# Two states of 64 channels per scan tile, with the scan results kept in PSUM

## The chip, the cores and the metric

The kernel runs on one core of one Trainium2 chip. A core has five engines, each with its own queue of instructions: TensorE (PE, matrix products), VectorE (DVE), ScalarE (ACT), GpSimd (POOL) and SyncE (SP, which here issues all DMAs). An engine executes its queue in order and waits at an instruction until the semaphores named in it have reached their values. Data live in SBUF and, for results of matrix products and some intermediates, in PSUM[...]. The metric is device time in microseconds.

## The reference, cut to what matters

Two layers are computed on four images of 384 channels and 32x32 positions. The first half of each layer is a state-space scan. For every channel d, with 16 states n:

```
dA = exp(dt[d, t] * A[d, n])
h[d, n] = h[d, n] * dA + dt[d, t] * u[d, t] * B[n, t]
y[d, t] = sum over n of h[d, n] * C[n, t]
```

Layer 0 does this in four directions over the image (rows, columns, and both reversed) on 384 channels; layer 1 does it once on 768 channels between an input projection with a short convolution and an output projection. Both have layer norms around them. The second half of layer 0 is a small feed-forward net; that of layer 1 is a mixture of four experts, computed densely.

## The kernel before, in words

Positions are the columns of a tile, channels its partitions. A *pass* is one direction (or one half of layer 1's channels) of one image on 512 positions: 384 channels as three chunks of 128 partitions. There are 48 passes. Half of them start a sequence ("first"), the other half continue from kept states. A pass has 16 *steps*, one for each state n, so there are 768 steps. A step consists of

- `times_b` on POOL (L834): s = dtu * bt for all three chunks, where dtu is dt*u and bt is row n of B, spread over the partitions by a DMA;
- three times `decay` on ACT (L839): da = exp(dt * A[:, n]) into one of two separate PSUM tiles `das`, used in turn;
- three times `scan` on DVE (L848), in place in s, with da as the factor;
- in first passes `keep_state` on DVE (L860), which copies the last column of the three chunks;
- `times_c`: the product with row n of C. DVE does the first `share` chunks (L883), reading C from the PSUM tile pc, which PE fills by a small product (`spread_c`, L864); POOL does the others (L894), reading C from the SBUF tile ct, filled by a DMA;
- three times `add` on PE (L874): acc[:, c] += identity * s[:, c], so that the sum over n builds up in PSUM.

There are five s tiles, three bt and three ct tiles. After 16 steps `gather` (DVE) takes acc out. `prep_pass` makes dt and dtu of a pass ahead of time, `project` makes the rows of B and C, and jobs called `prep0`, `post0`, `prep1`, `post1` do the layer norms, projections and the feed-forward net of each image beside the scans ("side work").

The order of all this on each engine is written out by a planner (`Plan.run`): it keeps a clock per engine, gives every operation a cost (for instance 0.63 for a decay, 1.18 for a scan) and dependences, and emits at each turn the operation that starts first. `choose` lets side work in where it is not expected to delay a scan. `split` chooses `share` from how far POOL is ahead. The order is fixed when the program is built. Semaphore waits are then put in by the tile framework, from which instruction writes and reads which tile; the planner's own dependences do not become waits.

After the last scan and `post1` of the last image comes `moe_layer`, the four experts, in plain program order; it isn't touched.

Of the kernel before, what the change touches and what calls it, by code (L numbers as in the profile page):

```python
# [11 lines left out]
BF16 = mybir.dt.bfloat16  # L12
# [6 lines left out]
P = 128  # L19
NB = 4  # L20
D = 384
NC = D // P
# [13 lines left out]
CROWS = (64, 96)  # L36
NQ = 112
# [183 lines left out]
def conv_layers(ctx, tc, ins, x2, const):  # L221
# [24 lines left out]
    wx1 = wp.tile([P, NI, NQ], F32, name="wx1")  # L246
# [7 lines left out]
    dts = tiles(2, [P, NC, T], "dt")  # L254
    dtus = tiles(2, [P, NC, T], "dtu")
    xds = tiles(2, [64, L], "xd")
    c3s = tiles(2, [NQ, L], "c3", BF16)
    dtws = tiles(2, [64, D], "dtw")
    wxs = tiles(2, [P, NC, NQ], "wx")
# [9 lines left out]
    das = tiles(2, [P, T], "da", pool=ps_1)  # L269
    pc = ps_1.tile([P, T], F32, name="pc")  # L270
# [14 lines left out]
    pick = wp.tile([NQ, NS], BF16, name="pick")  # L285
    nc.vector.tensor_copy(pick, ident[:NQ, :NS])
    for at in CROWS:
        nc.vector.tensor_tensor(pick, pick, ident[:NQ, at : at + NS], ALU.add)

    a0 = wp.tile([P, 4 * NC, NS], F32, name="a0")  # L290
    a1 = wp.tile([P, NI, NS], F32, name="a1")
# [19 lines left out]
    def part(dram_ap, c, h):  # L311
        return dram_ap[c * P : (c + 1) * P, cols(h)]
# [45 lines left out]
    def project(q, h, px):  # L358


        xd, c3 = q["xd"], q["c3"]
        lo, hi = CROWS
        yield ACT, 0.6
        nc.scalar.copy(c3[:, cols(h)], px[:NQ])
        yield ACT, 0.6
        nc.scalar.copy(xd[:, cols(h)], px[:64])
        yield DVE, 0.65
        nc.vector.tensor_tensor(px[lo:NQ], px[lo:NQ], c3[lo:NQ, cols(h)], ALU.subtract)
        yield ACT, 0.6
        nc.scalar.copy(c3[lo:NQ, cols(h)], px[lo:NQ])  # L370
        yield DVE, 0.65
        nc.vector.tensor_tensor(c3[hi:NQ, cols(h)], px[hi:NQ], c3[hi:NQ, cols(h)], ALU.subtract)  # L372
        ps.give(px)
# [7 lines left out]
    def prep_pass(q, h, slot, u, u_view):  # L381

        dt, dtu = dts[slot], dtus[slot]
# [18 lines left out]
        for c in range(NC):  # L402
            yield POOL, 1.35
            nc.gpsimd.tensor_tensor(u_view(dtu[:, c, :]), u_view(dt[:, c, :]), u[:, c], ALU.mult)  # L404

# [21 lines left out]
    def prep_quad0(q, b, k):  # L427
        def gen():
# [4 lines left out]
            for h in range(NT):  # L433
                px = yield from ps.take(True)
                yield PE, 2.75
                at = u[:, :, cols(h)] if k % 2 == 0 else turned(u, h)
                for c in range(NC):
                    nc.tensor.matmul(px[:NQ], lhsT=q["wx"][:, c, :], rhs=at[:, c], start=c == 0, stop=c == NC - 1)  # L438
                yield from project(q, h, px)
# [5 lines left out]
    def prep_pass0(q, b, k, h, slot):  # L445
        def gen():
            u = st[("u0", b)]
            if k % 2 == 0:
                yield from prep_pass(q, h, slot, u[:, :, cols(h)], lambda t: t)
            else:  # L450
                yield from prep_pass(q, h, slot, turned(u, h), lambda t: t.rearrange("p (w h) -> p w h", h=HW))

        return gen
# [17 lines left out]
    def post0(b):  # L471
# [15 lines left out]
        def add_x(h):  # L487
            def gen():
                for c in range(NC):
                    xh = yield from t1.take()  # L490
                    yield SP, LOAD
                    nc.sync.dma_start(out=xh, in_=part(x_in[b], c, h))
# [141 lines left out]
    def prep_quad1(q, b, g):  # L634
        def gen():
# [6 lines left out]
            for h in range(NT):  # L642
                px = yield from ps.take(True)
                yield PE, 5.5
                for c in range(NI):
                    nc.tensor.matmul(
                        px[:NQ], lhsT=wx1[:, c, :], rhs=xc[c // NC][:, c % NC, cols(h)], start=c == 0, stop=c == NI - 1
# [7 lines left out]
    def prep_pass1(q, b, g, h, slot):  # L655
        def gen():
            xc = st[("xc", b)][g]
            yield from prep_pass(q, h, slot, xc[:, :, cols(h)], lambda t: t)
# [10 lines left out]
    def post1(b):  # L669
# [28 lines left out]
        def out(h):  # L698
            def gen():
# [21 lines left out]
                for m in range(NC):  # L721
                    xh = yield from t1.take()
                    yield SP, LOAD
                    nc.sync.dma_start(out=xh, in_=part(x1[b], m, h))
# [19 lines left out]
    for m, (layer, b) in enumerate(order):  # L744
# [4 lines left out]
        for k, h, first, rev in of:  # L749
            if first:  # L750
                shared = st.get((1, b, 0)) if layer == 1 else None
                if not shared:
# [7 lines left out]
                    "c3": shared["c3"] if shared else c3s[n_quads % 2],  # L760
# [31 lines left out]
    for p, (m, layer, b, k, h, first, rev) in enumerate(passes):  # L792
# [6 lines left out]
        deps = [("quad", p if first else p - 1)] + ([("gather", p - 2)] if p > 1 else [])  # L799
        jobs.append((("pass", p), deps, p, [of_pass(q, b, k, h, p % 2)]))  # L800
# [24 lines left out]

    def load(i, of, ring):
        p, n = steps[i]
        nc.sync.dma_start(
            out=ring[i % len(ring)], in_=quad(p)["rows"][of + n : of + n + 1, cols(passes[p][4])].partition_broadcast(P)
        )  # L830

    def times_b(i):
        p, n = steps[i]
        nc.gpsimd.tensor_tensor(ss[i % NSR], dtus[p % 2], rep(bts[i % NBR]), ALU.mult)  # L834

    def decay(i, c):
        p, n = steps[i]
        q = quad(p)
        nc.scalar.activation(  # L839
            das[(NC * i + c) % 2], dts[p % 2][:, c, :], AF.Exp, scale=q["a"][:, q["c0"] + c, n : n + 1]  # L840
        )

    def scan(i, c):
        p, n = steps[i]
        _, _, _, _, _, first, rev = passes[p]
        way = slice(None, None, -1) if rev else slice(None)
        s = ss[i % NSR]
        nc.vector.tensor_tensor_scan(  # L848
            s[:, c, way],
            das[(NC * i + c) % 2][:, way],  # L850
            s[:, c, way],
            0.0 if first else state[:, n, c : c + 1],
            ALU.mult,
            ALU.add,
        )

    def keep_state(i):
        p, n = steps[i]
        last = 0 if passes[p][6] else T - 1
        nc.vector.tensor_reduce(state[:, n, :], ss[i % NSR][:, :, last : last + 1], AX.X, ALU.max)  # L860

    def spread_c(i):
        p, n = steps[i]
        nc.tensor.matmul(  # L864
            pc,
            lhsT=pick[:, n : n + 1].to_broadcast([NQ, P]),
            rhs=quad(p)["c3"][:, cols(passes[p][4])],
            start=True,
            stop=True,
        )  # L870

    def add(i, c):
        n = steps[i][1]
        nc.tensor.matmul(acc[:, c, :], lhsT=ident, rhs=ss[i % NSR][:, c, :], start=n == 0, stop=n == NS - 1)  # L874
# [5 lines left out]
    def times_c(i):  # L880
        m = share[i]
        s = ss[i % NSR]
        nc.vector.tensor_tensor(s[:, :m, :], s[:, :m, :], rep(pc, m), ALU.mult)  # L883
        plan.end["split", i] = 0.0
        for c in range(m):
            plan.end["part", i, c] = plan.end["mult", i]
        if m == NC:
            plan.skip.add(("c", i))
            plan.end["c", i] = plan.end["mult", i]

    def times_c_pool(i):
# [3 lines left out]
        for c in range(m, NC):  # L895
            plan.end["part", i, c] = plan.end["c", i]

    main, gathers, decays, bs, cs, pcs, bl, cl = ([] for _ in range(8))
    adds = [[] for _ in range(NC)]
    where = {}  # L900
    for i in range(N):
        p, n = steps[i]
        first = passes[p][5]
        after = ("state", i) if first else ("scan", i, 2)
        ring = [("add", i - NSR, c) for c in range(NC)] if i >= NSR else []
        bl.append(Op(("bt", i), LOAD, [("quad", p if first else p - 1)] + ([("b", i - NBR)] if i >= NBR else []), lambda i=i: load(i, NS, bts)))
        cl.append(Op(("ct", i), LOAD, [("quad", p if first else p - 1)] + ([("c", i - NCR)] if i >= NCR else []), lambda i=i: load(i, 0, cts)))
        bs.append(Op(("b", i), 3.42, [("pass", p), ("bt", i), *ring], lambda i=i: times_b(i)))
        for c in range(NC):
            x = NC * i + c - 2  # L910
            decays.append(
                Op(("da", i, c), 0.63, [("pass", p)] + ([("scan", x // NC, x % NC)] if x >= 0 else []), lambda i=i, c=c: decay(i, c))
# [389 lines left out]
```

## Time and profile before

| | |
|---|---|
| median of 3 runs | 6793.34 us (6784.1 to 6800.1) |
| profiled execution | 6791.07 us, span 6789.3 us |
| first scan starts, last scan starts | 79.7 us, 4503.0 us |
| DVE busy | 4097.3 us, 60% of the span |
| POOL busy | 4095.7 us, 60% |
| PE busy | 5920.9 us, 87% |
| ACT busy | 2838.5 us, 42% |
| DMA | 494.99 MB, 24.3% of 16 engines' span |

The span has two parts. To about 4.5 ms the scans run; then, up to 6.79 ms, the experts keep PE busy without a break while DVE and POOL stand nearly still. Shares of the whole span are therefore means over two stages. In a row of a group the first number after the bar is busy time in us, the second the mean length of one instruction in ns, and after the second bar stands the idle time of the engine just before these instructions, with what ended it.

### The profile page before, as it was taken

Reading aid. Unit: us, or ns where it says so; the run is one execution under the profiler, and the core shown is the slowest. Engines: PE = TensorE matmul, PEld = TensorE weight load, DVE = VectorE, ACT = ScalarE, POOL = GpSimd, SP = SyncE. Lnnn points to the kernel's source line nnn. Section 1 sums busy time; section 2 is a strip of 40 time slices with the busy share of each in tenths; the row PEclk is TensorE's granted clock in tenths of the full one; section 3 lists DMA queues with packets and bytes.
Section 4 is the critical chain, followed back from the end, with each engine's and each line's share of the span. In section 5 each row is a group of like instructions: output and inputs, shape, how many; then the busy total and the mean of one; then the engine's idle time right before and its main releaser. Section 6 shows DMA issues by size and latency. Waiting matters only on the chain. (4 is left out here: it accounts for less than half of the span.)

```text
span 6789.3 us, 43235 instructions
## 1 busy us (share of the span) xinstructions
PE 5920.9 (87%) x13120; PEld 2424.6 (36%) x13120; DVE 4097.3 (60%) x4047; ACT 2838.5 (42%) x3991; POOL 4095.7 (60%) x1760
## 2 busy tenths in 40 slices
PE   6777798978888987888897898877899999999999
PEld 2222233323333332333333233333444444444444
DVE  6999888898999889899988884951100000000000
ACT  4445565656555555655555555542211111111111
POOL 5999988998989788999988884960000000000000
PEclk8999999999999999999999899998899999999999
DMA  3333323333334333333433332423000000000000
GB/s 91 104 103 104 100 88 100 97 108 98 107 102 122 101 93 106 99 109 109 120 99 94 98 92 62 123 76 114 0 0 0 28 0 0 28 0 0 10 14 14
DMA packets 302859, 494.99 MB, mean 73 GB/s; under 512 B 38240, under 2 KB 82336, under 8 KB 302624
## 3 DMA queue, kind: packets, MB, share of 16 engines
q1 hardware_dynamic: 302624, 492.22, 24.3%
q8 instruction: 103, 1.69, 0.1%
q14 instruction: 132, 1.08, 0.1%
HBM read 470.61 MB, written 21.50 MB: 72 GB/s over the span
## 5 line engine op out<-in xcount | busy, mean ns | idle before, releaser
L834 POOL TENSOR_TENSOR s<-dtu,bt 128x1536 f32<-128x1536 f32 x768 | 2638.5, 3444 | 169.5 <-PE acc L874 95.7
L874 PE MATMUL acc<-s,ident 128*128 128x512 f32 x4608 | 2296.1, 630 | 122.7 <-POOL s L894 110.6
L839 ACT ACTIVATE da<-dt,a 128x512 f32<-128x512 f32 x2304 | 1580.3, 690 | 1608.1 <-DVE s L848 1605.2
L874 PEld LDWEIGHTS acc<-s,ident 128*128 128x128 f32 x4608 | 895.5, 199 | 1870.3 <-issue 1525.3
L848 DVE TENSOR_TENSOR_SCAN s<-da,state,s 128x512 f32<-128x512 f32 x1152 | 1401.6, 1266 | 119.4 <-ACT da L839 104.0
L848 DVE TENSOR_TENSOR_SCAN s<-da,s 128x512 f32<-128x512 f32 x1152 | 1336.5, 1206 | 168.1 <-ACT da L839 115.3
L1201 POOL TENSOR_TENSOR xb<-xb,yg 128x1536 f32<-128x1536 f32 x32 | 119.1, 3723 | 1835.5 <-DVE yg L1198 1776.6
L894 POOL TENSOR_TENSOR s<-s,ct 128x512 f32<-128x512 f32 (+1 forms) x698 | 1058.9, 1518 | 218.2 <-issue 110.3
L1198 DVE SCALAR_TENSOR_TENSOR yg<-py,pvt,gate 128x512 f32<-128x512 f32 x96 | 66.2, 745 | 1850.4 <-PE py L1175 1848.2
L1175 PE MATMUL py<-hid,w 128*128 128x512 f32 x2304 | 1048.1, 593 | 1.1 <-DVE yg L1198 1.1
L1187 PE MATMUL ph<-tb,w 128*128 128x512 f32 x2304 | 1046.6, 592 | 0.0
L883 DVE TENSOR_TENSOR s<-s,pc 128x1024 f32<-128x1024 f32 (+2 forms) x768 | 882.2, 1149 | 61.9 <-PE pc L864 20.5
L1191 ACT ACTIVATE hid<-ph,pvt 128x512 f32<-128x512 f32 x384 | 263.8, 687 | 1521.5 <-PE ph L1187 1514.0
L864 PE MATMUL pc<-c,pick 112*128 112x512 bf16 x768 | 303.6, 395 | 537.1 <-DVE s L883 534.6
L1175 PEld LDWEIGHTS py<-hid,w 128*128 128x128 f32 x2304 | 438.5, 190 | 555.2 <-issue 551.5
L1187 PEld LDWEIGHTS ph<-tb,w 128*128 128x128 f32 x2304 | 438.1, 190 | 552.2 <-issue 552.0
L580 PE MATMUL ps<-u,w 128*128 128x512 f32 x576 | 274.7, 622 | 12.6 <-DMA w<-in_w_in_dram 5.6
L388 PE MATMUL ps<-xd,dtw 12*128 12x512 f32 (+1 forms) x288 | 184.1, 734 | 29.4 <-ACT dt L397 14.3
L404 POOL TENSOR_TENSOR dtu<-dt,u 128x512 f32<-128x512 f32 x96 | 132.4, 1400 | 76.5 <-ACT dt L400 76.5
L580 PEld LDWEIGHTS ps<-u,w 128*128 128x128 f32 x576 | 114.0, 200 | 167.2 <-issue 137.7
L864 PEld LDWEIGHTS <-pick 112*128 112x128 bf16 x768 | 77.2, 100 | 236.7 <-issue 236.7
L438 PE MATMUL ps<-u,wx 128*112 128x512 f32 x192 | 140.8, 881 | 14.1 <-DVE c L372 7.8
(138 smaller groups left out, 3222.1 us busy)
## 6 DMA issues: line engine op xcount, KB each, us to landing
bt<-rows SPq DMA_DIRECT2D x768, 256.0 KB, 3.2
ct<-rows SPq DMA_DIRECT2D x768, 256.0 KB, 3.3
w<-in_w_dram SPq DMA_DIRECT2D x8, 2304.0 KB, 22.5
w<-in_w_in_dram SPq DMA_DIRECT2D x48, 192.0 KB, 3.7
w<-in_w_out_dram SPq DMA_DIRECT2D x48, 192.0 KB, 3.6
u<-in_x_dram SPq DMA_DIRECT2D x8, 768.0 KB, 8.5
t<-in_x_dram SPq DMA_DIRECT2D x24, 256.0 KB, 3.8
x<-yx SPq DMA_DIRECT2D x8, 768.0 KB
```

The costliest lines, as they stand in the source:

```text
L388: nc.tensor.matmul(pd, lhsT=q["dtw"][QROW : QROW + nr, c * P : (c + 1) * P], rhs=q["xd"][QROW : QROW + nr, cols(h)], start=True, stop=True,)
L580: nc.tensor.matmul(pi, lhsT=w[:, c, :], rhs=u[:, c, cols(h)], start=c == 0, stop=c == NC - 1)
L834: nc.gpsimd.tensor_tensor(ss[i % NSR], dtus[p % 2], rep(bts[i % NBR]), ALU.mult)
L839: nc.scalar.activation(das[(NC * i + c) % 2], dts[p % 2][:, c, :], AF.Exp, scale=q["a"][:, q["c0"] + c, n : n + 1])
L848: nc.vector.tensor_tensor_scan(s[:, c, way], das[(NC * i + c) % 2][:, way], s[:, c, way], 0.0 if first else state[:, n, c : c + 1], ALU.mu ...
L864: nc.tensor.matmul(pc, lhsT=pick[:, n : n + 1].to_broadcast([NQ, P]), rhs=quad(p)["c3"][:, cols(passes[p][4])], start=True, stop=True,)
L874: nc.tensor.matmul(acc[:, c, :], lhsT=ident, rhs=ss[i % NSR][:, c, :], start=n == 0, stop=n == NS - 1)
L883: nc.vector.tensor_tensor(s[:, :m, :], s[:, :m, :], rep(pc, m), ALU.mult)
L894: nc.gpsimd.tensor_tensor(s[:, m:, :], s[:, m:, :], rep(cts[i % NCR], NC - m), ALU.mult)
L1175: nc.tensor.matmul(py[:, m, :], lhsT=w2[:, f, m * P : (m + 1) * P], rhs=hid, start=f == 0, stop=f == NF - 1,)
L1187: nc.tensor.matmul(ph, lhsT=w1[:, c, f * P : (f + 1) * P], rhs=ts[i][:, c, :], start=c == 0, stop=c == NC - 1)
L1191: nc.scalar.activation(hid, ph, AF.Gelu, bias=pv("b1", e * NF + f))
```

## The change

A scan tile of 128 partitions now holds two states of 64 channels instead of one state of 128 channels: partitions 0 to 63 have state 2m, partitions 64 to 127 state 2m+1. A pass has six groups of 64 channels; its 16 steps are two *parts* of eight: part 0 does groups 0 to 2 and part 1 groups 3 to 5, each for the eight pairs of states m. So a step still has three chunks x of 512 columns, and there are still 768 steps.

- `prep_pass` makes dt and dtu in the old layout (one tile each, shared by all passes) and copies them by DMA, SBUF to SBUF, into tiles dts and dtus with each group of 64 channels written twice: eight DMAs for each part, 16 for a pass.
- `load` takes two DMAs of 64 partitions for a bt or ct tile, one for each state.
- The three decays of a step go to the three parts of one PSUM tile `da`, which has three banks and exists once. The scan writes its result over da in PSUM (`in_psum`), and DVE multiplies it with ct from SBUF into s (`times_c`). Chunks that POOL multiplies are scanned into s as before[...].
- A step on DVE is now scan 0, scan 1, (state), product of the first chunks, scan 2, (state), and, where `share` is 3, a second product. `keep_state` is called twice a step in first passes.
- `add` uses `both`, a 128x64 matrix that sums the two halves, and writes 64 partitions of acc.
- `pc`, `spread_c` and the bfloat16 rows c3 that it needed are gone; `project` is one copy on ACT instead of three on ACT and two on DVE.

```diff
-    das = tiles(2, [P, T], "da", pool=ps_1)
-    pc = ps_1.tile([P, T], F32, name="pc")
+    da = ps_1.tile([P, NC, T], F32, name="da")
...
+    both = wp.tile([P, HP], F32, name="both")
+    nc.vector.tensor_tensor(both, ident[:, :HP], ident[:, HP:], ALU.add)
...
     def project(q, h, px):
+        nr = QROW + q["rank"]
         yield ACT, 0.6
-        nc.scalar.copy(c3[:, cols(h)], px[:NQ])
-        yield ACT, 0.6
-        nc.scalar.copy(xd[:, cols(h)], px[:64])
-        yield DVE, 0.65
-        nc.vector.tensor_tensor(px[lo:NQ], px[lo:NQ], c3[lo:NQ, cols(h)], ALU.subtract)
-        yield ACT, 0.6
-        nc.scalar.copy(c3[lo:NQ, cols(h)], px[lo:NQ])
-        yield DVE, 0.65
-        nc.vector.tensor_tensor(c3[hi:NQ, cols(h)], px[hi:NQ], c3[hi:NQ, cols(h)], ALU.subtract)
+        nc.scalar.copy(q["xd"][:nr, cols(h)], px[:nr])
         ps.give(px)
...
+    def until(*keys):
+        while not all(k in plan.end for k in keys):
+            yield None
+        return max(plan.end[k] for k in keys)
...
+        for part in range(2):
+            before = 0.0
+            if p:
+                before = yield from until(("scan", NS * (p - 1) + 8 * part + 7, 2))
+            for to, of in ((dts[part], dt), (dtus[part], dtu)):
+                yield SP, LOAD, before
+                for side in range(2):
+                    mine = [x for x in range(NC) if (3 * part + x) % 2 == side]
+                    chunks = [(3 * part + x) // 2 for x in mine]
+                    for k in range(2):
+                        nc.sync.dma_start(
+                            out=to[k * HP : (k + 1) * HP, mine[0] : mine[-1] + 1 : 2, :],
+                            in_=of[side * HP : (side + 1) * HP, chunks[0] : chunks[-1] + 1, :],
+                        )
+            plan.end["pass", p, part] = plan.now + LOAD + 2.0
...
     def load(i, of, ring):
-        p, n = steps[i]
-        nc.sync.dma_start(
-            out=ring[i % len(ring)], in_=quad(p)["rows"][of + n : of + n + 1, cols(passes[p][4])].partition_broadcast(P)
-        )
+        p, part, m = place(i)
+        for k in range(2):
+            row = of + 2 * m + k
+            nc.sync.dma_start(
+                out=ring[i % len(ring)][k * HP : (k + 1) * HP, :],
+                in_=quad(p)["rows"][row : row + 1, cols(passes[p][4])].partition_broadcast(HP),
+            )
...
-    def decay(i, c):
+    def decay(i, x):
...
-        nc.scalar.activation(
-            das[(NC * i + c) % 2], dts[p % 2][:, c, :], AF.Exp, scale=q["a"][:, q["c0"] + c, n : n + 1]
-        )
+        g = 2 * q["c0"] + 3 * part + x
+        nc.scalar.activation(da[:, x, :], dts[part][:, x, :], AF.Exp, scale=q["a"][:, g, m : m + 1])
...
-        s = ss[i % NSR]
+        s = ss[i % NSR][:, x, way]
+        d = da[:, x, way]
+        in_psum = x < share[i] if x else True
         nc.vector.tensor_tensor_scan(
-            s[:, c, way],
-            das[(NC * i + c) % 2][:, way],
-            s[:, c, way],
-            0.0 if first else state[:, n, c : c + 1],
-            ALU.mult,
-            ALU.add,
+            d if in_psum else s, d, s, 0.0 if first else state[:, j, x : x + 1], ALU.mult, ALU.add
         )
...
-        nc.tensor.matmul(acc[:, c, :], lhsT=ident, rhs=ss[i % NSR][:, c, :], start=n == 0, stop=n == NS - 1)
+        nc.tensor.matmul(
+            acc[side * HP : (side + 1) * HP, c, :],
+            lhsT=both,
+            rhs=ss[i % NSR][:, x, :],
+            start=m == 0,
+            stop=m == NS // 2 - 1,
+        )
...
-        nc.vector.tensor_tensor(s[:, :m, :], s[:, :m, :], rep(pc, m), ALU.mult)
+        nc.vector.tensor_tensor(ss[i % NSR][:, lo:hi, :], da[:, lo:hi, :], rep(cts[i % NCR], hi - lo), ALU.mult)
...
         for x in range(NC):
+            free = [("da free", i - 1) if x == 2 else ("mult", i - 1, 0)] if i else []
+            decays.append(Op(("da", i, x), 0.63, [("pass", p, part), *free], lambda i=i, x=x: decay(i, x)))
+            main.append(
+                Op(("scan", i, x), 1.12 if first else 1.18, [("da", i, x), ("b", i)], lambda i=i, x=x: scan(i, x))
+            )
+            if x == 0:
+                continue
+            if first:
+                main.append(Op(("state", i, x - 1), 0.12, [], lambda i=i, x=x: keep_state(i, x - 1)))
+            main.append(Op(("mult", i, x - 1), 1.11 if x == 1 else 0.62, [("ct", i)], lambda i=i, x=x: times_c(i, x - 1)))
```

## The prediction

> **What bounds the kernel now.** I read the page's slices first: DVE and POOL are at 8 to 9 tenths up to slice 27 and then nearly still, PE is at 9 to the end. So there is a scan stage and an expert stage, and only the scan stage is touched. The groups and the waits come next, then the timeline of a few steps. First the groups (the page's part 5) of a step's instructions:
>
> ```profile
> L834 POOL TENSOR_TENSOR s<-dtu,bt 128x1536 f32<-128x1536 f32 x768 | 2638.5, 3444 | 169.5 <-PE acc L874 95.7
> L839 ACT ACTIVATE da<-dt,a 128x512 f32<-128x512 f32 x2304 | 1580.3, 690 | 1608.1 <-DVE s L848 1605.2
> L848 DVE TENSOR_TENSOR_SCAN s<-da,state,s 128x512 f32<-128x512 f32 x1152 | 1401.6, 1266 | 119.4 <-ACT da L839 104.0
> L848 DVE TENSOR_TENSOR_SCAN s<-da,s 128x512 f32<-128x512 f32 x1152 | 1336.5, 1206 | 168.1 <-ACT da L839 115.3
> L864 PE MATMUL pc<-c,pick 112*128 112x512 bf16 x768 | 303.6, 395 | 537.1 <-DVE s L883 534.6
> ```
>
> ACT sits idle 1605 us for scans, DVE only 219 us for decays: the decays run ahead of DVE. The chain of waits says the same pair by pair:
>
> ```profile
> ACT da L839 <- DVE s L848: 1605.2, 1731, 7.7
> DVE s L848 <- ACT da L839: 219.3, 111, 6.4
> DVE s L848 <- POOL s L834: 66.5, 18, 22.3
> ```
>
> Lines of the timeline, DVE and then ACT:
>
> ```profile
> 1822.95 1.20 DVE L883 TENSOR_TENSOR s<-s,pc 128x1024 f32<-128x1024 f32 x1
> 1824.06 3.63 DVE L848 TENSOR_TENSOR_SCAN s<-da,state,s 128x512 f32<-128x512 f32 x3
> 1827.61 1.19 DVE L883 TENSOR_TENSOR s<-s,pc 128x1024 f32<-128x1024 f32 x1
> ```
>
> ```profile
> 1825.38 0.69 ACT L839 ACTIVATE da<-dt,a 128x512 f32<-128x512 f32 x1 [1.61 <-DVE s L848]
> 1826.55 0.69 ACT L839 ACTIVATE da<-dt,a 128x512 f32<-128x512 f32 x1 [0.48 <-DVE s L848]
> 1827.72 0.69 ACT L839 ACTIVATE da<-dt,a 128x512 f32<-128x512 f32 x1 [0.48 <-DVE s L848]
> ```
>
> The reader is to see that DVE has no hole: the product starts 0.08 us before the record of the scan ahead of it ends, and each decay is made while DVE scans the other da tile. A step takes 4.66 us here. DVE is the bound, POOL close behind it. Over the scan stage (79.7 to 4504 us, 4424 us) there are about 100 us in which all wait for the side work of the last image, and some 330 us of other waits on DVE.
>
> [...] The three parts of the new da are three banks, so the chip would let ACT fill one while DVE scans another, as the trace shows with the two old da tiles; any wait between parts comes from the program. [...] The trace prices it: an independent operation starts 0.083 us before the end of the one ahead, one that waits for it 0.034 us after (state behind scan: 2614.08 to 2614.11), or 0.11 where the wait stands in an instruction of its own.
>
> **The change part by part.** The deciding view is not in the trace of before. It is the list of waits in the program built from the changed kernel, beside that of the old one. In the old program decay 0 of a step waits for scan 1 of the step before, decay 1 for its scan 2, decay 2 for scan 0 of its own step; these are the scans that last read the same da tile, and each scan waits for its own decay only. In the new program the waits go by the whole tile da, not by its parts, and follow the order in which the planner happened to emit:
>
> - decay 0 waits for scan 2 of the step before in 730 of 768 steps (the planner meant the product ahead of it);
> - decay 1 waits for decay 0 in 736;
> - decay 2 waits for scan 0 of its own step in 699;
> - scan 0 waits for decay 1, not just decay 0, in 618 (in most of the others the same wait stands at a neighbouring instruction, scan 2 or state or second product);
> - scan 1 waits for decay 2 in 712.
>
> So DVE and ACT take turns. Scan 0: 0.034 us from scan end to decay start (median of all cases in the trace where ACT was idle), 0.692 the decay, 0.032 to the next (as between dependent ACT operations, L337 to L338), 0.692, 0.10 to the scan: a hole of **1.55 us**. Scan 1: 0.034 + 0.692 + 0.034 = a hole of **0.76 us**. Neither is hidden by anything of the step, since both stand between two operations of DVE. Queued behind the held scan is all of DVE; behind the held decay, ACT's side work.
>
> Step by kind, with the groups' means (product of two chunks 1.208, of one 0.680, state 0.157). Continued pass, share 2: 3 x 1.266 + 1.55 + 0.76 + 1.208 + 0.07 (product waits for scan 1) - 0.083 = 7.30. First pass, share 2: 3 x 1.206 + 1.55 + 0.76 + 0.034 + 0.157 + 1.208 - 2 x 0.083 = 7.16; its second state falls into the hole. Share 1 is 0.528 shorter. Share 3 has its second product (0.68) after the decays are waited for: about 7.95. Counted in the built program: continued 269, 78 and 37 of shares 2, 1 and 3; first 244, 87 and 53. Sum 269 x 7.30 + 78 x 6.775 + 37 x 7.95 + 244 x 7.16 + 87 x 6.63 + 53 x 7.95 = **5533 us**.
>
> Added to it:
> - 1461 of 2304 scans write PSUM. No scan of before does. Products: 686 ns into PSUM (L346), 669 and 680 into SBUF (L565, L883). I take 20 ns, 29 us. [...]
> - ACT's side work, by its place in the built order with the durations of before. After decay 2 stand 676 us, 35 of them in the chain gap; there ACT is free for about 3.6 us a step, and 74 us stick out. Between decays 0 and 1 stand 60 us, all in the hole. Between 1 and 2 stand 98 us under scan 0 (1.25 us), 55 stick out. Sum 189; bounds 60 and 400, as inputs come early or late.
> - DVE's side work: 292 us. What stands ahead of scan 0, scan 1 or the second state is wholly or partly in a hole (102 us hidden); 190 us are not. Bounds 100 and 292.
> - The chain gap: fewer side operations are left for it in the built order (ACT 47 against 62, PE 38 against 90 apart from the adds and pc), so 70 instead of 100 us. ACT held by side inputs: 40 (0 to 100).
>
> The scan stage becomes 5533 + 29 + 189 + 190 + 70 + 40 = 6050 us, against 4424.
>
> Edits that I cost at nothing on this path, and their cover. `project` loses 80 DVE operations (57 us busy); its two subtractions are off the side work counted above. pc goes, 304 us of PE, which waited 535 us for DVE anyway. The adds stay 2304 products of 512 columns; where the trace has fewer columns (L546, 32), a half still takes 626 ns against 630; should the two halves of the array overlap, PE gains where it is no bound. POOL's 768 products with B stay and those with C go from 857 to 843 chunks; 5.2 us a step with its side work, under 7.2, so it falls off the bound. SP issues 4116 DMAs instead of 1812, 0.32 us each, 0.7 ms more over 6 ms. The repacking moves 48 x 3.1 MB = 151 MB; each part has eight steps, 57 us, to land. Its bursts of eight stand in SP's queue ahead of bt and ct loads; a ct load takes 3.4 us from issue to landing, and in the old order 7.6 us or more lie between its release and scan 1 in 99 of 100 steps. If that cover went, each late load would cost up to 5 us, 96 times at most. The start is 6 us longer (repacking, less the shorter project), the 2285 us after the last scan stay.
>
> Span: 80 + 6 + 6050 + 2285 = **8420 us**; the run is 2 us above its span, and the median 2 us above the profiled run, so 8420 for the median too.
>
> **Rivals.**
> 1. *Not slower: the decays still run ahead.* The mechanism: decays 0 and 1 are released by the product at the end of scan 1, and made under scan 2 (1.2 us), as the planner has it. Then DVE pays 60 us for more states, 105 for more waits on its own last operation, 20 for products and 29 for PSUM; it gains 57 and 37 (idle before L368 and L372, outside the gap) from `project`, up to 120 of the 219 us of late decays (ACT's longest free stretch grows from 2.1 to 3.3 us with three parts) and 30 of the gap: about **6765**. It decides if decay 0 starts at least 0.83 us before scan 2 ends. For it speaks the trace (ACT has 1605 us to spare); against it, that the built program has 730 waits for scan 2.
> 2. *The holes swallow the side work*: with both kinds of side work at their low bounds and no other waits, 80 + 6 + 5533 + 60 + 100 + 50 + 2285 = **8110**.
> 3. *Side work and loads add fully*: ACT in order between decays waits for PE and DVE, and the bursts make loads late: [...] **9130**, with 8700 on the way.
>
> **How the numbers follow.** Forecast 0.80 (range 8240 to 8600), rival 1 0.04, rival 2 0.09, rival 3 0.07. A range of 8130 to 8660 takes in most of rival 2 and the near part of rival 3. Faster by over 0.2%: 0.03, all of it rival 1; within 0.2% (about what a measurement can tell): 0.01; slower: 0.96.
>
> **What would show it.** Right: ACT's decays idle before scans and DVE's scans idle before decays both in the order of 1500 us and more, on nearly all of 1500 scans, with 1.55 and 0.76 us; a step of 7.2 us in the timeline; DVE and POOL at 6 to 7 tenths; the expert stage 2.15 ms as before. Wrong: scans idle for loads of ct or for POOL, or decays starting under scan 2. The sum would be off if dependent ACT operations take longer than 0.032 us to follow[...].

## The result and the profile after

The changed kernel takes 8374.61 us (median of 4 runs, 8369.96 to 8377.85) against 6793.35 us for the kernel before: a ratio of 1.2328, 95% interval 1.2307 to 1.2350. The forecast was 8420 us (8130 to 8660), slower with a chance of 0.96.

The profiled execution has a span of 8368.1 us against 6789.3. The first scan starts at 68.6 us (79.7 before), the last ends at 6086.5 (4504.3), and 2281.6 us follow (2285.0). So the scan stage grew from 4424.6 to 6017.9 us and nothing else grew. The groups of the page of after that answer to those shown of before:

```profile
L891 PE MATMUL acc<-s,both 128*64 128x512 f32 x4608 | 2420.1, 892 | 1841.5 <-DVE s L905 1575.4
L855 POOL TENSOR_TENSOR s<-dtus,bt 128x1536 f32<-128x1536 f32 x768 | 2630.6, 3433 | 214.0 <-PE acc L891 115.5
L861 ACT ACTIVATE da<-dts,a 128x512 f32<-128x512 f32 x2304 | 1593.4, 692 | 3310.5 <-DVE s L870 1879.6
...
L870 DVE TENSOR_TENSOR_SCAN da<-da,state,s 128x512 f32<-128x512 f32 x727 | 938.9, 1291 | 776.9 <-ACT da L861 743.7
...
L870 DVE TENSOR_TENSOR_SCAN da<-da,s 128x512 f32<-128x512 f32 x734 | 903.8, 1231 | 796.7 <-ACT da L861 553.5
...
L870 DVE TENSOR_TENSOR_SCAN s<-da,state,s 128x512 f32<-128x512 f32 x425 | 541.9, 1275 | 57.2 <-ACT da L861 56.6
```

The operations hardly got dearer: a decay takes 692 ns (690), POOL's product 3433 (3444), a scan of a second pass 1275 to 1291 (1266). What grew is the third column, the idle time ahead of decays and scans. Pair by pair, in the chain of waits of after (us in total, times, longest):

```profile
ACT da L861 <- DVE s L870: 1879.6, 606, 4.9
ACT da L861 <- DVE da L870: 1361.7, 790, 6.4
DVE da L870 <- ACT da L861: 1297.2, 1099, 5.9
...
DVE s L870 <- ACT da L861: 112.4, 133, 5.5
```

Before, ACT waited for scans for 1605 us and DVE for decays for 219. Now ACT waits 3241 us (both upper lines) and DVE 1410: each waits for the other. One step of the timeline, a first pass with share 2, DVE and then ACT (start, duration, and in brackets the idle time ahead):

```profile
2319.22 1.22 DVE L905 TENSOR_TENSOR s<-da,ct 128x1024 f32<-128x1024 f32 x1
2320.36 1.21 DVE L870 TENSOR_TENSOR_SCAN s<-da,s 128x512 f32<-128x512 f32 x1
2321.61 0.15 DVE L886 TENSOR_REDUCE state<-s 128x1 f32<-128x1 f32 x1
2323.12 1.23 DVE L870 TENSOR_TENSOR_SCAN da<-da,s 128x512 f32<-128x512 f32 x1 [1.36 <-ACT da L861]
2325.11 1.23 DVE L870 TENSOR_TENSOR_SCAN da<-da,s 128x512 f32<-128x512 f32 x1 [0.76 <-ACT da L861]
```

```profile
2321.61 1.42 ACT L861 ACTIVATE da<-dts,a 128x512 f32<-128x512 f32 x2 [2.77 <-DVE s L870]
2324.39 0.69 ACT L861 ACTIVATE da<-dts,a 128x512 f32<-128x512 f32 x1 [1.37 <-DVE da L870]
```

Decays 0 and 1 (one line, x2) start at 2321.61, when scan 2 has ended, though the product that last read their parts of da ended at 2320.44. Scan 0 starts when both are done. Decay 2 starts when scan 0 has ended, and scan 1 when decay 2 has. Before, DVE had no hole in such a step.

Added up over DVE's records between the first scan and the last: scans, products and states were busy for 3791 us before and 3921 after, side work for 365 and 315, the gaps between records came to 493 and 1909, and the overlaps (an operation starting ahead of the end of the one before) to 224 and 127. That is +130, -50, +1416 and +97: together 1593 us, the whole growth. Of the gaps of after, the net sum ahead of scan 0 is 1069 us, median 1.42 us, and ahead of scan 1 it is 568 us, median 0.76.

### The profile page after: what moved, and what is told of

Read it like the earlier page. It is cut to its first block, busy times and chain, and to the rows that moved or that the text cites. A ratio compares the mean times of both kernels' runs of the same rounds, so it can differ in the third digit from the quotient of the medians.

```text
span 8368.1 us, 46296 instructions
## 1 busy us (share of the span) xinstructions
PE 6121.9 (73%) x12352; PEld 1949.0 (23%) x12352; DVE 4267.1 (51%) x4439; ACT 2823.2 (34%) x3911; POOL 4084.6 (49%) x1740
## 5 line engine op out<-in xcount | busy, mean ns | idle before, releaser
L891 PE MATMUL acc<-s,both 128*64 128x512 f32 x4608 | 2420.1, 892 | 1841.5 <-DVE s L905 1575.4
L855 POOL TENSOR_TENSOR s<-dtus,bt 128x1536 f32<-128x1536 f32 x768 | 2630.6, 3433 | 214.0 <-PE acc L891 115.5
L861 ACT ACTIVATE da<-dts,a 128x512 f32<-128x512 f32 x2304 | 1593.4, 692 | 3310.5 <-DVE s L870 1879.6
L870 DVE TENSOR_TENSOR_SCAN da<-da,state,s 128x512 f32<-128x512 f32 x727 | 938.9, 1291 | 776.9 <-ACT da L861 743.7
L891 PEld LDWEIGHTS acc<-s,both 128*64 128x64 f32 x4608 | 464.7, 180 | 3692.7 <-DVE s L905 2166.8
L870 DVE TENSOR_TENSOR_SCAN da<-da,s 128x512 f32<-128x512 f32 x734 | 903.8, 1231 | 796.7 <-ACT da L861 553.5
L905 DVE TENSOR_TENSOR s<-da,ct 128x1024 f32<-128x1024 f32 (+1 forms) x858 | 910.8, 1061 | 70.0 <-ACT da L861 47.9
L870 DVE TENSOR_TENSOR_SCAN s<-da,state,s 128x512 f32<-128x512 f32 x425 | 541.9, 1275 | 57.2 <-ACT da L861 56.6
L870 DVE TENSOR_TENSOR_SCAN s<-da,s 128x512 f32<-128x512 f32 x418 | 507.6, 1214 | 57.2 <-ACT da L861 55.8
L627 PE MATMUL ps<-tmp,w 128*128 128x512 f32 x288 | 156.4, 685 | 27.0 <-ACT yx L631 17.6
```

The lines of the kernel that those rows point to most:

```text
L627: nc.tensor.matmul(pk, lhsT=taps[tap], rhs=xt[:, tap + h * T : tap + (h + 1) * T], start=tap == 0, stop=tap == 3)
L855: nc.gpsimd.tensor_tensor(ss[i % NSR], dtus[place(i)[1]], rep(bts[i % NBR]), ALU.mult)
L861: nc.scalar.activation(da[:, x, :], dts[part][:, x, :], AF.Exp, scale=q["a"][:, g, m : m + 1])
L870: nc.vector.tensor_tensor_scan(d if in_psum else s, d, s, 0.0 if first else state[:, j, x : x + 1], ALU.mult, ALU.add)
L891: nc.tensor.matmul(acc[side * HP : (side + 1) * HP, c, :], lhsT=both, rhs=ss[i % NSR][:, x, :], start=m == 0, stop=m == NS // 2 - 1,)
L905: nc.vector.tensor_tensor(ss[i % NSR][:, lo:hi, :], da[:, lo:hi, :], rep(cts[i % NCR], hi - lo), ALU.mult)
```

## The experiments

Three theories were to be told apart. **Theory 1**, the forecast's: the waits go by the whole PSUM tile da. **Theory 2**: a result kept in da until the product has read it leaves ACT too little time, whatever the tile. **Theory 3**: the half-column adds, the doubled loads or the repacking hold the kernel. All times in one table; a ratio is to the runs of the kernel before on the same chip. In the table a bank stands for the 512 float32 columns that one part of da has.

| kernel | channels | PSUM tiles for da | DVE's scan results | C for DVE | us | ratio (95%) |
|---|---|---|---|---|---|---|
| before | 128 | two of one bank | SBUF | PSUM | 6793 | 1 |
| after | 64 | one of three banks | PSUM | SBUF | 8374.6 | 1.2328 (1.2307 to 1.2350) |
| e1_three | 64 | three of one bank | PSUM | SBUF | 6747.7 | 0.9932 (0.9915 to 0.9948) |
| e2_pair | 64 | one of two, one of one | PSUM | SBUF | 7088.3 | 1.0434 (1.0419 to 1.0450) |
| e3_before_one | 128 | one of two banks | SBUF | PSUM | 7657.4 | 1.1271 (1.1254 to 1.1288) |
| e4_before_c3 | 128 | three of one bank | SBUF | SBUF | 7294.6 | 1.0741 (1.0726 to 1.0756) |
| e5_before_c2 | 128 | two of one bank | SBUF | SBUF | 7398.8 | 1.0891 (1.0876 to 1.0906) |
| e7_128_channels | 128 | three of one bank | PSUM | SBUF | 6713.2 | 0.9887 (0.9872 to 0.9902) |
| e8_states_on_act | 64 | three of one bank | PSUM | SBUF | 6786.8 | 0.9991 (0.9985 to 0.9998) |

(e6_same_half, one run, is below.)

**e1_three.** The same PSUM banks, cut into three tiles:

```diff
-    da = ps_1.tile([P, NC, T], F32, name="da")
+    das = tiles(NC, [P, T], "da", pool=ps_1)
...
-        nc.vector.tensor_tensor(ss[i % NSR][:, lo:hi, :], da[:, lo:hi, :], rep(cts[i % NCR], hi - lo), ALU.mult)
+        for x in range(lo, hi):
+            nc.vector.tensor_tensor(ss[i % NSR][:, x, :], das[x], cts[i % NCR], ALU.mult)
```

> The changed kernel with its da cut into three PSUM tiles, one bank each, so that no wait can cover more than one part. Everything else of the change stays: 64 channels to a state, results kept in PSUM, C from SBUF, half-column adds, repacking, two row loads of half height. The price of the cut: the product of two chunks becomes two of one (2 x 0.68 - 0.083 against 1.208, +0.07 us in about 600 steps, 42 us) and a first pass has three state operations for two (some 50 us). Theory 1 (the waits go by the whole tile): decay 0 is released by its own product, decay 1 by the next, both are made under scan 2 (1.2 us), decay 2 under scans 0 and 1, so both holes close: a step of 4.8 to 4.9 us, the gaps ahead of scans 0 and 1 near 0 where they were 1.42 and 0.76 us, scan stage 4424 + 29 + 42 + 50 - 60 = about 4490, the whole 6840 us (6750 to 6950). Theory 2 (keeping the results in da until the product has read them leaves ACT too little time, whatever the tile): decay 0 starts behind the product in either case and the hole ahead of scan 0 stays at half its size or more, 7500 us or more. Theory 3 (half-column adds, twice the loads or the repacking hold the kernel): unchanged, 8300 to 8450.

Measured: 6747.65 us. The whole loss is gone, and the kernel is 0.7% faster than before. The chain of waits of e1_three:

```profile
ACT da L861 <- DVE s L907: 1276.7, 653, 8.1
...
ACT da L861 <- DVE s L870: 200.0, 412, 5.2
...
DVE da L870 <- ACT da L861: 180.0, 103, 5.9
```

Decays now wait for the product (L907), the operation that the planner meant, and DVE's wait for decays fell from 1410 to some 200 us (these 180, and 23 ahead of scans into s). Its timeline, DVE and then ACT, in a second pass:

```profile
2304.15 1.26 DVE L907 TENSOR_TENSOR s<-da,ct 128x512 f32<-128x512 f32 x2
2305.33 1.27 DVE L870 TENSOR_TENSOR_SCAN s<-da,state,s 128x512 f32<-128x512 f32 x1
2306.52 2.44 DVE L870 TENSOR_TENSOR_SCAN da<-da,state,s 128x512 f32<-128x512 f32 x2
```

```profile
2304.85 1.30 ACT L861 ACTIVATE da<-dts,a 128x512 f32<-128x512 f32 x2 [0.71 <-DVE s L907]
2306.64 0.69 ACT L861 ACTIVATE da<-dts,a 128x512 f32<-128x512 f32 x1 [0.48 <-DVE s L870]
```

Decay 0 starts at 2304.85, behind the first of the two products, and both decays are done at 2306.15 under scan 2 (2305.33 to 2306.60). Theories 2 and 3 fall: everything that they name is still there. The estimate of 6840 was 92 us too high: scans, products and states took 238 us more than before (products and states 111 or 112 each, scans 15), but overlaps rose by 142, since most operations start some 0.08 to 0.09 us before the one ahead ends; side work and gaps fell by 50 and 66. The scan stage is 4404.6 us, 20 less than before, where I had 4490.

**e2_pair.** Parts 0 and 1 in one tile, part 2 in another:

```diff
-    da = ps_1.tile([P, NC, T], F32, name="da")
+    da01 = ps_1.tile([P, 2, T], F32, name="da01")
+    da2 = ps_1.tile([P, 1, T], F32, name="da2")
```

> The changed kernel with parts 0 and 1 in one PSUM tile of two banks and part 2 in its own: the product of two chunks and the state stay one operation each. Theory 1 foretells each hole by itself: scan 1 waits for scan 0 instead of decay 2, so its hole of 0.76 us goes. Decays 0 and 1 are both released by the product, ahead of scan 2, but scan 0 still waits for decay 1: 0.034 + 0.692 + 0.032 + 0.692 + 0.10 = 1.55 us after the product's end, of which scan 2 covers 1.19, so a hole of 0.36 us (0.42 in first passes) stays ahead of scan 0. A step 1.85 us shorter than in the changed kernel, 768 x 1.85 = 1420: about 6950 us (6900 to 7150). Theory 2: 7500 or more. Theory 3: 8300 to 8450.

Measured: 7088.25 us. Of the timeline of e2_pair:

```profile
2302.04 1.23 DVE L910 TENSOR_TENSOR s<-da,ct 128x1024 f32<-128x1024 f32 x1
2303.18 1.27 DVE L875 TENSOR_TENSOR_SCAN s<-da,state,s 128x512 f32<-128x512 f32 x1
2304.80 2.62 DVE L875 TENSOR_TENSOR_SCAN da<-da,state,s 128x512 f32<-128x512 f32 x2 [0.35 <-ACT da L866]
```

The hole ahead of scan 1 is gone (median gap 0.035 us), and the one ahead of scan 0 is 0.35 us (median over the trace 0.346; 0.36 was worked out). The median step became 1.91 us shorter than in the changed kernel (7.38 to 5.47), as expected, but the mean step only 1.67 (7.84 to 6.17): 0.24 x 767 = some 185 us, more than the 138 us between 6950 and 7088. Both kernels have the same side work in the same steps. The 326 steps with none on DVE and ACT became 1.98 us shorter (mean), the 441 with some only 1.43. So the holes had covered side work that stands in the way again.

**e3_before_one.** The kernel before, with its two da tiles made one:

```diff
-    das = tiles(2, [P, T], "da", pool=ps_1)
+    pair = ps_1.tile([P, 2, T], F32, name="da")
+    das = [pair[:, k, :] for k in range(2)]
```

> The kernel before with nothing changed but that its two da tiles become one PSUM tile of two banks. Theory 1: the waits now go by that tile. In the built program decay 0 waits for scan 2 of the step before (655 of 768 steps), decay 1 for decay 0, scan 0 for decay 1 (738), decay 2 for scan 1 (702) and scan 2 for decay 2 (630) or decay 0 of the next step (94). Ahead of scan 0 the same 1.55 us as in the changed kernel run from the end of scan 2, but the product (1.21, started 0.08 early) covers 1.13 of it: a hole of about 0.42. Ahead of scan 2 a hole of 0.76 (about 1.5 in the 94). Step + (0.42 + 0.083) + (0.76 + 0.083) = 1.35 us, 768 x 1.35 + 94 x 0.7 = 1100: about 7890 us (7650 to 8100). Theories 2 and 3 have no part in this kernel: 6793.

Measured: 7657.39 us, so this alone costs 865 us in a kernel that has nothing else of the change. From its chain of waits:

```profile
ACT da L840 <- DVE s L849: 2560.7, 1396, 8.5
...
DVE s L849 <- ACT da L840: 1002.7, 1117, 7.8
```

The holes have the sizes that were worked out: medians of 0.41 us ahead of scan 0 and 0.76 ahead of scan 2. Their sum was put too high: over the kernel before, the net gaps ahead of scan 0 grew by 271 us and those ahead of scan 2 by 597, 868 instead of 1100, since in 4 of 10 steps next to nothing is left ahead of scan 0 (0.035 us or less). Most of these are in first passes, where the median there is 0.033 us against 0.44 in second ones: the state and its waits stand there beside the product, and together they cover nearly all of the 1.55 us. The cause stands; the count of steps that pay for it was the error.

**e6_same_half.** Do adds into the two halves of acc's partitions run at the same time, and does it matter?

```diff
-        c, side = divmod(3 * part + x, 2)
+        c, side = x, part
```

> The changed kernel with the sums of a part of 8 steps all put into one half of TensorE's columns (part 0 into the lower, part 1 into the upper; the channels come out in another order, so the sums land in other places) instead of alternating. It asks whether products into the two halves run at the same time. The trace of the changed kernel has records of two neighbouring adds 7 ns apart, and then the next two 480 ns later: if the halves run together, the busy time of the adds, 2420 us, grows by some 30 to 70% here; if they don't, it stays within 5%. In both cases the time stays at 8374 within 30 us by theory 1, since TensorE is not the bound; by theory 3 (the adds hold the kernel) it would grow with the adds, by 500 us or more.

Measured: 8380.38 us in one run, 6 us from the changed kernel. One line of the timeline of PE in after, and one in e6_same_half; each is two adds, and an add has two records (4608 for the 2304 adds):

```profile
2312.27 1.08 PE L891 MATMUL acc<-s,both 128*64 128x512 f32 x4 [0.97 <-DVE s L905]
```

```profile
2301.49 1.93 PE L891 MATMUL acc<-s,both 128*64 128x512 f32 x4 [1.57 <-DVE s L905]
```

Two adds take 1.08 us when they go to different halves, and 1.93 when they go to the same one. The granted clock was 1.0 in the first stretch; the second is too short for 0.5, since the records of adds in before start 0.43 us apart at 1.0 and 0.85 at 0.5 (medians). In the first the records come in pairs that start 6 ns apart, so there the two adds do run at the same time. The busy time of the adds rose from 2420 to 2878 us, 19%, less than the 30% expected; the mean granted clock of the two runs differs too (0.771 and 0.851), so that ratio is no clean measure of the overlap. For the time it is worth nothing: with 458 us more of adds the kernel takes as long.

**e4_before_c3 and e5_before_c2.** Since C from SBUF frees the bank of pc, a third da tile can stand in the old kernel. One takes C from SBUF with three da tiles, the other with two:

```diff
-    das = tiles(2, [P, T], "da", pool=ps_1)
-    pc = ps_1.tile([P, T], F32, name="pc")
+    das = tiles(3, [P, T], "da", pool=ps_1)
...
-        nc.vector.tensor_tensor(s[:, :m, :], s[:, :m, :], rep(pc, m), ALU.mult)
+        nc.vector.tensor_tensor(s[:, :m, :], s[:, :m, :], rep(cts[i % NCR], m), ALU.mult)
```

> The kernel before with one part of the change alone: C multiplied from SBUF (ct, which POOL's share of the product reads already), so pc, its 768 products on TensorE and the splitting of C in project go; the PSUM bank of pc holds a third da tile of its own. States keep 128 channels, scans write SBUF, adds use all columns, no repacking. In the built program each decay now waits for the scan three before it: decay 0 for scan 0 of the step before, and so on. Theory 1 (the wait structure decides, and da in tiles of their own leaves DVE no holes): DVE loses 57 us of project and up to 120 of the 219 us in which scans wait for decays; scan stage 4424 - 57 - 100 = about 4270, the whole 6640 us (6600 to 6720), which is below the changed kernel with three tiles (6748). Rival: a product with both inputs in SBUF takes longer than 1.208 us while POOL works on SBUF too, or slows POOL: 0.1 us a step would be 77 us, 0.2 us would eat the gain (6790).

> As the one with C from SBUF and three da tiles, but with the two da tiles of the kernel before: it parts the gain of the third tile from that of C. Theory 1: only the 57 us of project on DVE and some of the wait of the products for pc (33 us of gaps) go, the late decays stay (219 us): 6720 us (6690 to 6770). If the third tile is worth nothing, both come out alike. If the product from SBUF is dear, both lose the same against this.

Measured: 7294.59 and 7398.77 us, far on the side of the rival. The third tile is worth 104 us of the 120 that were put down for it, but the product from two SBUF operands costs far more. A group of DVE and one of POOL in before, then DVE's groups of e4_before_c3, each shape apart, and POOL's:

```profile
L883 DVE TENSOR_TENSOR s<-s,pc 128x1024 f32<-128x1024 f32 x539 | 651.2, 1208 | 40.5 <-PE pc L864 13.6 <-DVE state L860 0.9 <-PE acc L874 0.5
L894 POOL TENSOR_TENSOR s<-s,ct 128x512 f32<-128x512 f32 x539 | 685.5, 1272 | 139.4 <-issue 89.1 <-POOL s L834 22.8 <-POOL s L894 10.0
```

```profile
L872 DVE TENSOR_TENSOR s<-s,ct 128x1024 f32<-128x1024 f32 x551 | 1229.3, 2231 | 9.4 <-DVE state L849 0.5
L872 DVE TENSOR_TENSOR s<-s,ct 128x1536 f32<-128x1536 f32 x120 | 329.0, 2742 | 4.1
L872 DVE TENSOR_TENSOR s<-s,ct 128x512 f32<-128x512 f32 x97 | 165.3, 1704 | 2.0
...
L883 POOL TENSOR_TENSOR s<-s,ct 128x512 f32<-128x512 f32 x551 | 1062.7, 1929 | 123.8 <-issue 102.8 <-DVE state L849 5.8 <-POOL dtu L393 5.0
```

A product of two chunks takes 2231 ns where it took 1208 with C in PSUM, and one of each other size is about 1.0 us longer as well (2742 for 1754, 1704 for 680); POOL's product of one chunk takes 1929 ns for 1272. One step of the timeline of e4_before_c3, DVE and then POOL:

```profile
1829.46 2.13 DVE L872 TENSOR_TENSOR s<-s,ct 128x1024 f32<-128x1024 f32 x1
```

```profile
1827.08 3.43 POOL L823 TENSOR_TENSOR s<-dtu,bt 128x1536 f32<-128x1536 f32 x1
1830.47 2.25 POOL L883 TENSOR_TENSOR s<-s,ct 128x512 f32<-128x512 f32 x1
```

DVE's product begins at 1829.46 while POOL's product with B runs until 1830.51, and it ends 1.08 us after that, at 1831.59. POOL's next product begins at 1830.47, while DVE's is at work, and ends 1.13 us after DVE's, at 1832.72. Both end about one microsecond later (0.93 and 0.99 us) than with the 1.20 and 1.26 us of such products that meet no operation of the other engine. It is so throughout the trace. 475 of the 551 products of two chunks begin while POOL is in the middle of an operation; each takes what was left of that operation and 1.08 us more (1.080 to 1.085 in 8 of 10). The other 76 take 1.20 us, as long as with C in PSUM. On POOL, the 377 products of one chunk that begin during one of DVE's end 1.13 us (median) after it, and the other 174 take 1.26. So C from SBUF isn't slow by itself; the product is dear where it meets an operation of the other engine. Why it is held there is not shown. The expectation had it as a rival of 0.1 to 0.2 us, the author's estimate; the trace has 1.0 us on the mean of DVE's products.

**e7_128_channels.** The same layout as e4_before_c3, C from SBUF, three da tiles, but the scan results that DVE multiplies kept in PSUM:

```diff
-        nc.vector.tensor_tensor(s[:, :m, :], s[:, :m, :], rep(cts[i % NCR], m), ALU.mult)
+        for x in range(lo, hi):
+            nc.vector.tensor_tensor(ss[i % NSR][:, x, :], das[x], cts[i % NCR], ALU.mult)
```

(`scan`, `keep_state`, the list of operations and `choose` are those of e1_three; `load`, `add`, `decay` and `prep_pass` those of the kernel before.)

> The 128-channel layout of the kernel before with the other half of the change: scan results kept in three da tiles in PSUM, C multiplied from SBUF, the same planner code as the changed kernel's with three tiles (e1_three). It differs from e1_three by the layout alone (no repacking, one row load instead of two of half height, adds over all columns), and from e4_before_c3 by where DVE's product finds its scan result: PSUM here, SBUF there. If the 1.04 us that DVE's two-chunk product had over 1.208 in e4_before_c3, and the 0.66 us that POOL's own had over 1.27, come from both engines reading two SBUF operands at a time, the product here takes 0.68 a chunk, POOL's 1.27, and the time is that of e1_three, 6748 us (6690 to 6800): the layout touches TensorE, SP and the DMA queues, none of which bounds the scan stage. If C from SBUF is dear by itself, 7300. If the 64-channel layout is worth something by itself, over 6800, and if its loads cost something, under 6690.

Measured: 6713.16 us, 581 us less than e4_before_c3. DVE's group, and POOL's:

```profile
L868 DVE TENSOR_TENSOR s<-da,ct 128x512 f32<-128x512 f32 x1541 | 993.9, 680 | 4.3
```

```profile
L880 POOL TENSOR_TENSOR s<-s,ct 128x512 f32<-128x512 f32 x503 | 638.0, 1269 | 160.7 <-issue 91.4 <-POOL s L823 30.5 <-DMA ct<-rows 11.1
```

With one operand in PSUM the product is back at 680 ns a chunk, and POOL's at 1269. So the two halves of the change's idea belong together in this kernel: C can come from SBUF at 680 ns a chunk because the scan result stays in PSUM. This is the fastest of all, 1.1% below the kernel before. Against e1_three it has the layout of 128 channels, and the ratios to the kernel before (0.9887 and 0.9932) have intervals that don't meet: the 64-channel layout, with the order and the shares that the planner makes of it, costs some 30 us. In the profiled executions, which are 44 us apart, the first scan starts 5 us later (70.3 against 65.1), the scan stage is 41 us longer (4404.6 against 4363.7) and the rest 3 us shorter. What in the stage it is was not pursued.

**e8_states_on_act.** e1_three with its states on ACT; the planner's cost for a state on DVE goes from 0.12 to 0.01:

```diff
-            nc.vector.tensor_reduce(state[:, j, x : x + 1], src, AX.X, ALU.max)
+            nc.scalar.copy(state[:, j, x : x + 1], src)
...
-                main.append(Op(("state", i, x - 1), 0.12, [], lambda i=i, x=x: keep_state(i, x - 1)))
+                main.append(Op(("state", i, x - 1), 0.01, [], lambda i=i, x=x: keep_state(i, x - 1)))
```

> The changed kernel with three da tiles (e1_three), and its 1152 state operations moved from DVE to ACT. A single state takes 0.15 us on DVE, less the 0.083 by which the next operation starts early: 77 us, and up to 163 where they stood in DVE's way with a wait. ACT has the time: 1499 us of idle ahead of decays in e1_three. But a state in ACT's queue stands between decays, and waits for its scan. Expected 6748 - 77 = about 6670 us (6600 to 6720); if DVE doesn't bound e1_three but POOL does (4078 us busy, 3.45 + 1.27 + side work a step), nothing is gained: 6730 to 6760; if ACT's order makes decays late, 6780 or more.

Measured: 6786.79 us, 39 more than e1_three. DVE did lose the 163 us of states, though the planner gave it 52 more products of one chunk (some 30 us). From the chain of waits of e8_states_on_act:

```profile
POOL s L919 <- ACT state L887: 184.9, 91, 7.9
...
DVE s L907 <- ACT state L887: 151.9, 141, 6.7
```

Two new waits of 337 us together stand against the saving: POOL's product writes over the chunk that the state has still to be read from, and in ACT's queue a state can stand behind side work. In sum over the scan stage, DVE's operations took 145 us less than in e1_three, its gaps came to 125 more, and 48 us of overlaps went: 28 us longer. How much of POOL's 185 us reaches DVE was not separated. Of the three outcomes written down it was the third, though by another door than decays: DVE waits for decays 159 us at scans into PSUM, no more than the 180 of e1_three.

## Why the prediction was right

**What decides.** The forecast did not follow the diff, in which each decay waits for the product that read its part, but the list of waits of the built program, where each wait goes by the whole tile. e1_three and e3_before_one show that this list was the cause: cutting the tile takes away all of the loss, and joining two tiles brings 865 us of it into a kernel without the change.

**The holes.** 0.76 us ahead of scan 1: median 0.759. 1.55 us ahead of scan 0: 1.54 in second passes, 1.36 in first ones, where the state stands in the hole as the forecast had it. Their parts (medians, the forecast's in brackets): decay 0 starts 0.035 us after scan 2 (0.034), decay 1 0.032 after decay 0 (0.032), scan 0 0.10 after decay 1 (0.10), decay 2 0.035 after scan 0 (0.034), scan 1 0.033 after decay 2 (0.034).

**The sum.** The scan stage came to 6018 us for 6050, closer than its parts. Steps without side work on DVE have medians of 7.39 us (continued) and 7.30 (first) with share 2, forecast as 7.30 and 7.16; 6.64 and 6.54 with share 1 (6.775 and 6.63); 8.26 and 8.20 with share 3 (7.95). With the counts of each kind they add up to some 5596 us, where the forecast had 5533, or 5562 with its 29 for scans into PSUM. For all the rest, side work on ACT and DVE, the chain gap and late inputs, that leaves 422 us where it had 489. The two errors partly cancelled, which is luck. The side-work terms (189, 190 and 40) were not measured one by one.

**Terms that were off.**
- *Chain gap, 70 us*: 91 us, in two waits of 11 and 80. In the built order I counted fewer side operations left for it. Its longest wait is 80 us here, 81 in e1_three, 79 in e2_pair and 73 in e7_128_channels, so among these it depends on neither holes nor steps; in the kernel before it was 57 and 22 in two pieces, in e4_before_c3 and e5_before_c2 55 and 17. Why is open.
- *The start, 6 us longer*: 11 shorter. The first scan starts at 63 to 65 us without repacking and with the short `project` (e4_before_c3, e5_before_c2, e7_128_channels), at 68 to 70 with both, and at 80 before. The shorter `project` was worth some 15 us there, the repacking cost 5.
- *PSUM-writing scans, 20 ns each*: 16 to 17 ns in after (1291 against 1275, 1231 against 1214), which looks right. In e1_three, where these scans are seldom held, they take 1270 against 1272, and 1219 against 1209. There the few that do start behind a wait take 1291 too, and the others 1269 (second passes). So most of the 16 ns belongs to scans that start behind a wait, and writing PSUM is worth 0 to 10 ns. The 20 ns were the author's estimate from products; no scan of before writes PSUM, so its trace could not show the price.

**Costed at nothing.** The adds, pc, repacking and loads stand as they were put, though an issue of SP took 0.59 us in after (median) for the 0.32 of the forecast: with 458 us more of adds (e6_same_half) the time stays within 6 us, and with all the loads and the repacking in place e1_three is faster than before.

**The rivals.** The first, that the decays run ahead, was given 6765 us and a chance of 0.04. It named what decides it: decay 0 starting under scan 2. That kernel is e1_three, at 6748. The second, that holes swallow side work, holds in part: e2_pair got some 185 us less from closing the holes than their size, and lost it in the steps with side work, where the forecast had left 102 us of DVE's hidden and priced ACT's by its place. The third, that late loads and all of the side work add up, did not come (its 9130 us, and the 5 us of a late load, were the author's estimates): in after DVE's products waited 0.7 us in all for loads of ct.

## What to carry to other kernels

When parts of a buffer are to be filled and emptied in turn by two engines, give each part a tile of its own, even if they lie side by side in memory; then look in the built program at what the first instruction of each part waits for, since the diff and the planner's own list of dependences show only what was meant. In this kernel a tile in three parts cost 1627 us over three tiles, with the same banks, instructions and bytes but for a split product and state.

Before an operand moves from PSUM to SBUF, look at where the other operand of that instruction is, and what the other engines do at that time: here the same product took 0.68 us a chunk with one operand in PSUM, and about 1.0 us more an instruction with both in SBUF beside POOL (e4_before_c3: 2.23 for two chunks, where before had 1.21).

## What the runs showed of the hardware

Three things stand out. In e4_before_c3, DVE's products with both inputs in SBUF and POOL's products took longer where they met: a product of two chunks on DVE ended 1.08 us after the POOL operation during which it began, and POOL's next one 1.13 us after DVE's (on the mean 2231 against 1208 ns on DVE for two chunks, 1929 against 1272 on POOL for one), which made a kernel with less work 7.4% slower. Adds into the two halves of acc's partitions ran two in 1.08 us (after) where two into the same half took 1.93 (e6_same_half). And the mean granted clock of TensorE differed: 0.947 before, 0.939 in e7_128_channels, 0.885 in e1_three, 0.771 in after. In these four it fell with the share of the scan stage in which TensorE was busy (83, 83, 77 and 65%), but that share alone does not account for it: e2_pair has 0.821 at 76%, e3_before_one 0.905 at 75%. What sets it is not shown. The time of after hardly depends on TensorE in this stage, since 458 us more of adds left it within 6 us (e6_same_half).
